# A planned four-layer graph kernel: new planning costs, groups of two at both ends, the last scores ranked ahead, and one late batch's variances on ScalarE

## The chip, the cores and the metric

The kernel runs on one core of a Trainium2 chip, in float32. The metric is device time in microseconds (us) of one execution; the time of a kernel is the median of its runs. The core's engines are TensorE (PE; its weight loads are listed as PEld), VectorE (DVE), ScalarE (ACT), GpSimd (POOL) and SyncE (SP), which here only issues transfers.

## The reference

There are 128 batches; each is a matrix x of 128 nodes by 512 features. All share one 128x128 adjacency matrix `adj`. Each batch passes through four layers, and each layer ends in a layer norm of x plus the layer's result:

```python
# layer 0: graph product
x = ln(x + (adj @ x) @ W0 + bias0)
# layer 1: graph attention; the mask multiplies the logits
h = x @ W;  s1, s2 = h @ a1, h @ a2
att = softmax(leaky_relu(s1[:, None] + s2[None, :], 0.2) * adj)
x = ln(x + elu(att @ h + beta * h))
# layer 2: max over features, one number for each node
A = adj @ x;  C = adj @ x + b
x = ln(x + max(relu(A[:, None, :] + (C - A)[:, :, None]), axis=-1))
# layer 3: 8 heads of 64, masked where adj is 0
q, k, v = split(x @ w_qkv)
o = softmax(where(adj == 0, -inf, q @ k.T / 8)) @ v
o = o @ w_proj + b_proj
x = ln(x + o + (o - mean(o)) * rsqrt(var(o) + eps) * gamma + beta)
```

So layer 3 has two norms, one of the projection `o` and one of the sum. A norm needs the mean and variance of 512 numbers in each of 128 rows, and a root.

## The kernel before, in words

**Data.** One batch is one 128x512 tile `x`; 18 tiles of it are in flight. The weights stay in SBUF. A 128x512 product is four matmuls over the inner dimension into one PSUM bank (`product`, L229), and each float32 matmul shows as two instructions, so a product is 8 instructions. PSUM has 5 banks named `mm` and 3 named `tr`.

**Layers 0 to 2** (`batch`). `mixed` (L237) multiplies x with the transposed adjacency or attention matrix into a `tr` bank; ScalarE copies the result to `yT` (L248) and `product` multiplies it with W0 or W. VectorE adds (L671, L696, L699), `bn_stats` and `bn_aggr` (L177, L183) give mean and variance, GpSimd raises variance plus eps to the power -0.5 (L191, `root`), and the normalise runs on ScalarE (L211) or VectorE (L216). Layer 2 is one matmul pair with adj (L706) and a maximum (L709). The attention weights of layer 1 are made for two batches at once (`attention1`), with trips through DRAM.

**Layer 3 works in groups** (`Group`): batches 0 to 115 in groups of four, 116 to 127 in six groups of two. When the x of a batch is done it is transposed by VectorE in blocks (L721) and taken through DRAM into the group's `xT` (`features`, four DMAs for each batch, L648). Once every batch of the group is there, `query_key` makes queries and keys for the whole group (L535; moving side 512 wide in a group of four, 256 in a group of two); ScalarE and VectorE copy them out (L544, L546). `tiled` then issues the score matmuls (L590) and, for groups of four, the attention matmuls of the group before (L611) in between; for the last groups each batch has its own score step and `attend` issues the attention matmuls. The softmax in between is mask add (L735), maximum (L742), eight exponentials on ScalarE (L746), a division (L753), a blocked transpose (L756) and two DMAs through DRAM (`p_d`). `values` makes v (a `product`). The attended rows are copied by ScalarE (L776) and projected. `usual` then does the two last norms: add of the bias (L795), statistics, two products on VectorE (L802, L805), statistics, normalise (L216), and the store from SP's queue (L809). `last` does the same for batch 127 in two half-width products (L824, L839, L840, L848, L854, L858, L863), so that its norm starts earlier.

**Slots.** `xT` and `qkT` (queries, keys, and then the softmax) have two slots each, one for each group; `v` has 8, `yT` 4, `ex` 2. The `xT` slot of a group comes free when its query-key work and all its `values` are done; the `qkT` slot when its attention matmuls are done.

**Order.** The order of every engine's queue is written out at build time by a planner in Python (`Plan`); on the chip each queue runs in that order, and an instruction waits for its inputs. Each step of a chain is requested with `use(engine, work, take, late, urgent, follow)`: the engine, the planned duration in us, the slots that it takes, what passes until its result may be used. The planner takes the request that can start first; among those that could start at the same time, `follow` goes before `urgent` before the rest, and then the lower rank:

```python
t, _, _, n = min(
    (self.at(r), r["want"][4], r["rank"], n) for n, r in enumerate(self.requests)
)
```

A TensorE request that is not `follow` is planned up to `MARGIN = 1.0` us after its inputs are ready. The rank is in general the batch's number (the group's first batch for group steps); `values` has its batch plus `LATER = 12`, and the layers 0 to 2 of the last 14 batches have 8 less. The planned durations do not exist on the chip: they only decide the order.

Of the kernel before, what the change touches and what calls it, by code (L numbers as in the profile page):

```python
# [8 lines left out]
F32 = mybir.dt.float32  # L9
# [7 lines left out]
D = 512  # L17
K = D // P
G = 4
PAIRS = 6  # L20
H = 8
HD = D // H
S = 32
# [22 lines left out]
class Plan:  # L46
# [15 lines left out]
    def use(self, engine, work, take=None, late=0.05, urgent=False, follow=False):  # L62

        names = take if callable(take) else lambda: (take,) if take else ()
        return engine, work, names, late, 0 if follow else 1 if urgent else 2
# [61 lines left out]
def gnn_stack_kernel(  # L131
# [40 lines left out]

    def mean_rstd(src):

        yield use("DVE", 1.03)
        st = small.tile([P, 6], F32, name="st")
        nc.vector.bn_stats(st, src)  # L177
        mv, ve = mean_var(st)
        return mv, (yield from root(ve))
# [14 lines left out]
    def beside(chain, rank):  # L194

        event, result = Event(), []

        def run():
            result.append((yield from chain))
            done(event)  # L200

        plan.start(run(), rank)
        return event, result

    def layernorm_act(xb):
        mv, rstd = yield from mean_rstd(xb)
# [24 lines left out]

    def mixed(xb, nodes, first=False):

        b0, b1 = yield use("PE", 0.91, lambda: ("tr", "yT"), late=0.2)
        p = bank([P, K, P], "tr")
        for k in range(K):
            nc.tensor.matmul(p[:, k, :], xb[:, k * P : (k + 1) * P], nodes, start=True, stop=True)  # L237
        yT = buf([P, K, P], "yT")
        if first:
            fill(2)  # L240

            yield use("DVE", 0.35, late=0.0)
            nc.vector.tensor_copy(yT[:, : K // 2], p[:, : K // 2])  # L243
            yield use("ACT", 0.05, urgent=True)
            nc.scalar.copy(yT[:, K // 2 :], p[:, K // 2 :])
        else:
            yield use("ACT", 0.6, urgent=True)
            nc.scalar.copy(yT, p)  # L248
        give(b0)
        return yT, b1  # L250
# [11 lines left out]
    make_identity(nc, ident)  # L262
    neghalf = const.tile([P, 1], F32, name="neghalf")
    nc.gpsimd.memset(neghalf, -0.5)
    adj_sb = const.tile([P, P], F32, name="adj_sb")
    adjT = const.tile([P, P], F32, name="adjT")

# [157 lines left out]

        return i - AHEAD if i >= NB - LAST else i

    quads = NB // G - PAIRS * 2 // G
    groups = {}

    def group(i):

        g = i // G if i < quads * G else quads + (i - quads * G) // 2
        if g not in groups:
            first, size = (g * G, G) if g < quads else (quads * G + (g - quads) * 2, 2)
            gr = groups[g] = Group(first, size)
            rank = first
            for h in range(size // 2):
                plan.start(attention1(gr, h), early(first + 2 * h))
            steps = K // gr.chunks  # L440
            for n in range(2 * steps):
                plan.start(query_key(gr, n // 2 * gr.chunks + K * (n % 2)), rank + n / K)


            if g < quads:
                plan.start(tiled(gr, groups.get(g - 1), range(size)), rank)
            else:
                for b in range(size):
                    plan.start(tiled(gr, None, (b,)), rank)
            if g >= quads - 1:  # L450
                for b in range(0, size, 2):
                    for bs in ((b, b + 1),) if g < quads + PAIRS - 1 else ((b,), (b + 1,)):
                        plan.start(attend(gr, bs), rank)
        return groups[g]


# [65 lines left out]
    def query_key(gr, c):  # L522
        yield gr.turned
        yield w3_in
        got = yield use("PE", 3.46, lambda: ("mm",) if gr.qkT else ("mm", "qkT"), late=0.2)
        if gr.qkT is None:
            bp, gr.slot["qkT"] = got
            gr.qkT = buf([P, G, 2 * K, P], "qkT")
        else:
            bp = got  # L530
        n = gr.chunks
        p = bank([P, n, gr.size * P], "mm")
        for j in range(n):
            for k in range(K):
                nc.tensor.matmul(  # L535
                    p[:, j, :], wqkv_sb[:, k, (c + j) * P : (c + j + 1) * P],
                    gr.xT[:, k, : gr.size * P], start=(k == 0), stop=(k == K - 1),
                )
        gr.read("xT", gr.size + 2 * K // n)
        yield use("ACT" if c < K else "DVE", 0.69, urgent=True)  # L540
        for j in range(n):
            dst = gr.qkT[:, : gr.size, c + j, :]
            if c < K:
                nc.scalar.mul(dst, p[:, j, :].rearrange("p (b n) -> p b n", b=gr.size), HD**-0.5)  # L544
            else:
                nc.vector.tensor_copy(  # L546
                    dst.rearrange("p b (c r) -> p b c r", c=Q),
                    p[:, j, :].rearrange("p (b r c) -> p b c r", b=gr.size, c=Q),
                )
        give(bp)  # L550
        done(gr.qk)

    def tiled(gr, before, bs):
        yield gr.qk
        waiting = list(range(before.size)) if before else []
        for b in waiting:
            yield before.rows[b]
        for n in range(0, len(bs), 2):

            now, then = bs[n : n + 2], waiting[: BUFS["tr"]]  # L560
            got = yield use(
                "PE", 0.1 + 0.88 * len(now) + 0.15 + 0.87 * len(then),
                lambda: ("mm", "mm") * len(now) + ("tr",) * len(then),
                late=0.0, urgent=True, follow=n > 0,
            )
            got = got if isinstance(got, list) else [got]
            for b in now:
                score(gr, b, got[:2])
                got = got[2:]
            if then:  # L570
                attends(before, then, got)

            for k, b in enumerate(now):
                done(
                    gr.scored[b],
                    0.15 - 0.88 * (len(now) - 1 - k) - (0.15 + 0.87 * len(then) if then else 0),
                )
            waiting = waiting[len(then) :]
            while waiting:
                got = yield use("PE", 0.88, "tr", late=0.0, follow=True)  # L580
                attends(before, waiting[:1], [got])
                waiting = waiting[1:]

# [12 lines left out]
    def attend(gr, bs):  # L596
        for b in bs:
            yield gr.rows[b]
        slots = yield use(
            "PE", 0.25 + 0.88 * len(bs), lambda: ("tr",) * len(bs), late=0.0, urgent=True  # L600
        )
        attends(gr, bs, slots if len(bs) > 1 else [slots])

# [17 lines left out]
    def values(i, gr, event):  # L621
        b = i - gr.first
        yield gr.turned
        bp, bv = yield use("PE", 3.46, lambda: ("mm", "v"), late=0.2)
        p = product(
            lambda k: gr.xT[:, k, b * P : (b + 1) * P], lambda k: wqkv_sb[:, k, 2 * D :]
        )
        yield use("ACT", 0.6, urgent=True)
        event.v = buf([P, D], "v")
        nc.scalar.copy(event.v, p)  # L630
        give(bp)
        gr.read("xT", gr.size + 2 * K // gr.chunks)
        event.slot = bv
        done(event)
# [19 lines left out]
    def batch(i):  # L654
# [8 lines left out]
        biased = Event()  # L663
        plan.start(pool_add(xb, bias0_sb, biased, bias0_in), i)
        yield w0_chunk[1]
        bp = yield use("PE", 3.46, "mm", late=0.2)
        p = product(lambda k: yT[:, k, :], lambda k: w0_sb[:, k, :])
        give(by)
        yield biased
# [15 lines left out]
        yield gr.attention[h]  # L685
        yT, by = yield from mixed(xb, gr.eT[h][:, b % 2])
        gr.read(h, 2)
        bp = yield use("PE", 3.46, "mm", late=0.2)
        p = product(lambda k: yT[:, k, :], lambda k: w1_sb[:, k, :])
        give(by)  # L690

# [9 lines left out]
        yield from layernorm_act(xb)  # L701


        bp = yield use("PE", 0.88, "mm", late=0.2, urgent=True)
        p = bank([P, D], "mm")
        nc.tensor.matmul(p, adjT, xb, start=True, stop=True)  # L706
        yield use("DVE", 0.69, urgent=True)
# [36 lines left out]
        for j in range(H):  # L744
# [31 lines left out]
        nc.scalar.copy(oT, p)  # L776
        give(ba)

        yield from (last if i == NB - 1 else usual)(
            i, xb, oT, valued, biased  # L780
        )

# [5 lines left out]

    def usual(i, xb, oT, valued, biased):

        bp = yield use("PE", 3.46, "mm", late=0.2)
        p = product(lambda k: oT[:, k, :], lambda k: wproj_sb[:, k, :])
        yield use("DVE", 0.69, urgent=True)
        o = valued.v
# [14 lines left out]
        nc.sync.dma_start(out[i], xb)  # L809
        give(x_slot[i])  # L810

    def last(i, xb, oT, valued, biased):

        halves = [slice(h * D // 2, (h + 1) * D // 2) for h in range(2)]
# [3 lines left out]

        def multiply():
            for h, columns in enumerate(halves):  # L820
                bp = yield use("PE", 1.73, "mm", late=0.0, follow=h > 0)
                p = bank([P, D // 2], "mm")
                for k in range(K):
                    nc.tensor.matmul(  # L824
                        p, oT[:, k, :], wproj_sb[:, k, columns], start=(k == 0), stop=(k == K - 1)
                    )
                banks.append((p, bp))
                done(multiplied[h], 0.2)
            give(valued.slot)
# [79 lines left out]
```

## Time and profile before

| | before |
|---|---|
| median of 4 runs | 3251.77 us (3251.59 to 3252.37) |
| the profiled execution, its own time | 3252.96 us |
| its span, first to last instruction | 3251.2 us, 40319 instructions |
| granted TensorE clock, mean | 0.999 |
| TensorE busy | 3234.8 us, 12767 matmul instructions |
| VectorE busy | 2670.1 us |
| ScalarE busy | 1186.2 us |
| GpSimd busy | 953.6 us |
| share of the DMA engines taken by the data queue | 30.8% |

In the lines of the profile, "L229" is line 229 of the kernel's file; a group's line gives engine, operation, `out<-in` by tile names, the count, the busy time and the mean duration of one in ns, and the idle time before the group with what ended it. TensorE's busy time is pipelined and its ends are modelled. The steps from the start of one matmul to the start of the next are the better measure of its pace: 0.429 us for a 512-wide instruction of a product, 0.216 for a 256-wide one. Some matmul records are missing from the trace.

### The profile page before, as it was taken

How to read it: one execution, taken by the hardware profiler on the slowest of the kernel's cores; microseconds unless marked ns; L12 is line 12 of the kernel's file. 1: busy time of each engine (PE TensorE's matmuls, PEld its weight loads, DVE VectorE, ACT ScalarE, POOL GpSimd, SP SyncE). 2: the span in 40 equal slices, each digit the busy share in tenths (PEclk: the TensorE clock that was granted, in tenths of full speed). 3: DMA queues.
4: the chain of work that ended last, by engine and by line, in shares of the span. 5: the costliest groups of instructions: out<-in, count | busy, mean ns of one | idle time of the engine just before them, and what ended most of it. 6: DMA issues, size and time to landing. Idle time of an engine off the chain costs nothing.

```text
span 3251.2 us, 40319 instructions
## 1 busy us (share of the span) xinstructions
PE 3234.8 (99%) x12767; PEld 1714.0 (53%) x12767; DVE 2670.1 (82%) x5671; ACT 1186.2 (36%) x3469; POOL 953.6 (29%) x1032
## 2 busy tenths in 40 slices
PE   9999999999999999999999999999999999999998
PEld 5455555555555555555555555555555555555565
DVE  7987797877978779787797877978779787878877
ACT  3343343423434333343333342334423333333332
POOL 3313232322323223232232322323223232322322
PEclk9999999999999999999999999999999999999999
DMA  5233332233322333223232232322333222332332
GB/s 172 69 90 101 99 101 94 61 103 98 102 91 61 107 94 105 94 58 104 94 110 90 61 101 94 113 87 64 98 94 115 88 70 78 115 106 72 93 111 85
DMA packets 469893, 304.27 MB, mean 94 GB/s; under 512 B 319280, under 2 KB 401584, under 8 KB 469680
## 3 DMA queue, kind: packets, MB, share of 16 engines
q1 hardware_dynamic: 469536, 301.42, 30.8%
q8 instruction: 102, 1.67, 0.2%
q14 instruction: 111, 0.91, 0.1%
q10 hardware_dynamic: 144, 0.26, 0.0%
HBM read 158.93 MB, written 142.67 MB: 93 GB/s over the span
## 4 chain that ended last, share of the span: by engine, by line
PE 98%; DVE 1%; DMA 0%; POOL 0%; issue 0%; ACT 0%; POOLq 0%; DVEq 0%; SPq 0%; ACTq 0%
PE mm L229 53%; PE mm L535 27%; PE tr L237 7%; PE mm L590 4%; PE tr L611 4%; PE mm L706 3%; DMA p_d<-pt 0%; DVE st L177 0%; DVE x L805 0%; DVE t L802 0%; DMA e_d<-et 0%; DVE x L216 0%; DVE pt L756 0%; DVE qkT L753 0%; POOL rstd L191 0%
## 5 line engine op out<-in xcount | busy, mean ns | idle before, releaser
L229 PE MATMUL mm<-w_sb,yT 128*128 128x512 f32 x2048 | 902.3, 592 | 0.2 <-DVE yT L243 0.2
L535 PE MATMUL mm<-xT,wqkv_sb 128*128 128x512 f32 (+1 forms) x2240 | 888.7, 556 | 0.0
L191 POOL TENSOR_TENSOR rstd<-ve,neghalf 128x1 f32<-128x1 f32 x640 | 438.1, 684 | 1148.8 <-DVE ve L185 952.5
L535 PEld LDWEIGHTS mm<-xT,wqkv_sb 128*128 128x128 f32 x2240 | 425.1, 190 | 455.6 <-issue 424.2
L229 PEld LDWEIGHTS mm<-w_sb,yT 128*128 128x128 f32 x2048 | 386.9, 190 | 475.5 <-issue 469.9
L229 PE MATMUL mm<-wqkv_sb,xT 128*128 128x512 f32 x1024 | 459.6, 593 | 0.0
L229 PE MATMUL mm<-wproj_sb,v 128*128 128x512 f32 x1016 | 444.4, 594 | 0.7 <-ACT v L776 0.7
L746 ACT ACTIVATE qkT<-qkT,nmx 128x128 f32<-128x128 f32 x1024 | 395.4, 390 | 40.0 <-DVE nmx L742 40.0
L222 POOL TENSOR_TENSOR x<-x,v 128x512 f32<-128x512 f32 x127 | 175.8, 1385 | 673.9 <-DVE v L795 672.1
L177 DVE BATCH_NORM_STATS2 st<-x 128x6 f32<-128x512 f32 x511 | 348.7, 682 | 4.8 <-ACT x L714 1.9
L229 PEld LDWEIGHTS mm<-wproj_sb,v 128*128 128x128 f32 x1016 | 191.2, 190 | 235.6 <-issue 230.3
L211 ACT ACTIVATE x<-x,nmr,rstd 128x512 f32<-128x512 f32 x256 | 205.3, 810 | 249.0 <-DVE nmr L209 245.9
L229 PEld LDWEIGHTS mm<-wqkv_sb,xT 128*128 128x128 f32 x1024 | 188.0, 190 | 203.7 <-issue 199.7
L544 ACT ACTIVATE qkT<-mm 128x512 f32<-128x512 f32 (+1 forms) x140 | 77.1, 560 | 558.1 <-PE mm L535 556.3
L222 POOL TENSOR_TENSOR x<-x,bias_sb 128x512 f32<-128x512 f32 x128 | 172.2, 1351 | 313.3 <-PE tr L237 303.6
L248 ACT COPY yT<-tr 128x512 f32<-128x512 f32 x255 | 148.5, 584 | 285.9 <-PE tr L237 285.8
L735 DVE TENSOR_TENSOR qkT<-mm,maskb 128x512 f32<-128x512 f32 x256 | 163.7, 684 | 80.1 <-PE mm L590 80.0
L222 POOL TENSOR_TENSOR x<-x,beta_sb 128x512 f32<-128x512 f32 x128 | 172.3, 1348 | 155.9 <-DVE xt L721 146.4
L678 DVE SCALAR_TENSOR_TENSOR scr<-x,wa_rows 128x512 f32<-128x512 f32 x256 | 194.9, 761 | 22.2 <-ACT x L211 17.5
L746 ACT ACTIVATION_READ_ACCUMULATOR qkT<-qkT,nmx 128x1 f32 x1024 | 194.4, 190 | 0.0
L694 ACT ACTIVATE ex<-mm 128x512 f32<-128x512 f32 x128 | 76.4, 597 | 299.3 <-PE mm L229 281.7
L630 ACT COPY v<-mm 128x512 f32<-128x512 f32 x128 | 74.9, 585 | 298.8 <-PE mm L229 298.2
(75 smaller groups left out, 3593.8 us busy)
## 6 DMA issues: line engine op xcount, KB each, us to landing
p_d<-pt SPq DMA_DIRECT2D x128, 512.0 KB
qkT<-p_d SPq DMA_DIRECT2D x128, 512.0 KB
x_d<-xt SPq DMA_DIRECT2D x128, 256.0 KB
xT<-x_d SPq DMA_DIRECT2D x512, 64.0 KB
x<-in_x SPq DMA_DIRECT2D x127, 256.0 KB
out<-x SPq DMA_DIRECT2D x127, 256.0 KB
z<-s_d SPq DMA_DIRECT2D x64, 128.0 KB
e_d<-et SPq DMA_DIRECT2D x64, 128.0 KB
```

Source lines behind the costliest of these rows:

```text
L177: nc.vector.bn_stats(st, src)
L191: nc.gpsimd.tensor_tensor(rstd, ve, neghalf, op=ALU.pow)
L211: nc.scalar.activation(xb, xb, AF.Identity, bias=nmr, scale=rstd)
L222: nc.gpsimd.tensor_tensor(dst, dst, other, op=ALU.add)
L229: nc.tensor.matmul(p, lhs(k), rhs(k), start=(k == 0), stop=(k == K - 1))
L237: nc.tensor.matmul(p[:, k, :], xb[:, k * P : (k + 1) * P], nodes, start=True, stop=True)
L248: nc.scalar.copy(yT, p)
L535: nc.tensor.matmul(p[:, j, :], wqkv_sb[:, k, (c + j) * P : (c + j + 1) * P], gr.xT[:, k, : gr.size * P], start=(k == 0), stop=(k == K - 1),)
L590: nc.tensor.matmul(p[j][:, c, :], gr.qkT[rws, b, c, :], gr.qkT[rws, b, K + c, :], start=True, stop=True,)
L678: nc.vector.scalar_tensor_tensor(scr, xb, 1.0, wa_rows[:, j, :], op0=ALU.mult, op1=ALU.mult, accum_out=gr.s[:, b, j : j + 1],)
L735: nc.vector.tensor_tensor(pr[:, j * K : (j + 1) * K], sc[j], maskb[:, None, :].to_broadcast([P, K, P]), op=ALU.add,)
L746: nc.scalar.activation(pr[:, j, :], pr[:, j, :], AF.Exp, bias=nmx[:, j : j + 1], accum_out=sums[:, j : j + 1],)
```

## The change

It has five parts.

1. The planned durations of TensorE steps are changed: a product from 3.46 to 3.44 us, `mixed` from 0.91 to 0.9, the 128x512 adjacency product and the score and attention steps from 0.88 to 0.87, and the statistics step on VectorE from 1.03 to 1.02.
2. The groups: two groups of two (batches 0 to 3), 29 groups of four (4 to 119), four groups of two (120 to 127).
3. The query-key and score steps of the last two groups (batches 124 to 127) get a rank lower by 8. Their attention steps keep theirs.
4. Batch 125 takes a new path, `late`, in place of `usual`: sums come from the `accum_out` of VectorE's products, the squares are summed by a `Square` on ScalarE, the last normalise runs on ScalarE, and the store is issued from ScalarE's queue.
5. A constant tile `eps` is set by GpSimd at the start.

The core of the diff (left out: lines where only a planned duration of part 1 changes):

```diff
-PAIRS = 6
+FIRST, PAIRS = 2, 4
+ENDING, SOON = 4, 8
...
+    def negated_mean(total):
+        nm = small.tile([P, 1], F32, name="nm")
+        nc.vector.tensor_scalar(nm, total, -1.0 / D, None, op0=ALU.mult)
+        return nm
+
+    def rstd_act(src, nm):
+
+        b = yield use("ACT", 1.2, "yT")
+        square = buf([P, D], "yT")
+        var = small.tile([P, 1], F32, name="var")
+        nc.scalar.activation(square, src, AF.Square, bias=nm, accum_out=var)
+        give(b)
+        ve = small.tile([P, 1], F32, name="ve")
+        nc.scalar.activation(ve, var, AF.Identity, bias=eps, scale=1.0 / D)
+        return (yield from root(ve, follow=True))
...
+    eps = const.tile([P, 1], F32, name="eps")
+    nc.gpsimd.memset(eps, EPS)
...
-    quads = NB // G - PAIRS * 2 // G
+    sizes = [2] * FIRST + [G] * ((NB - 2 * (FIRST + PAIRS)) // G) + [2] * PAIRS
+    firsts = [sum(sizes[:g]) for g in range(len(sizes))]
+    group_of = [g for g, size in enumerate(sizes) for _ in range(size)]
...
-        g = i // G if i < quads * G else quads + (i - quads * G) // 2
+        g = group_of[i]
         if g not in groups:
-            first, size = (g * G, G) if g < quads else (quads * G + (g - quads) * 2, 2)
+            first, size = firsts[g], sizes[g]
             gr = groups[g] = Group(first, size)
-            rank = first
+            rank = first - (SOON if first >= NB - ENDING else 0)
...
-            if g < quads:
+            joined = len(sizes) - PAIRS
+            if g < joined:
                 plan.start(tiled(gr, groups.get(g - 1), range(size)), rank)
             else:
                 for b in range(size):
                     plan.start(tiled(gr, None, (b,)), rank)
-            if g >= quads - 1:
+            if g >= joined - 1:
                 for b in range(0, size, 2):
-                    for bs in ((b, b + 1),) if g < quads + PAIRS - 1 else ((b,), (b + 1,)):
-                        plan.start(attend(gr, bs), rank)
+                    for bs in ((b, b + 1),) if g < len(sizes) - 1 else ((b,), (b + 1,)):
+                        plan.start(attend(gr, bs), first)
...
-        yield from (last if i == NB - 1 else usual)(
+        yield from (last if i == NB - 1 else late if i == NB - 3 else usual)(
             i, xb, oT, valued, biased
         )
...
+    def late(i, xb, oT, valued, biased):
+
+        bp = yield use("PE", 3.44, "mm", late=0.2)
+        p = product(lambda k: oT[:, k, :], lambda k: wproj_sb[:, k, :])
+        yield use("DVE", 0.92, late=0.0, urgent=True)
+        o = valued.v
+        total = small.tile([P, 2], F32, name="total")
+        nc.vector.scalar_tensor_tensor(
+            o, p, 1.0, bproj_sb, op0=ALU.mult, op1=ALU.add, accum_out=total[:, 0:1]
+        )
+        nm = negated_mean(total[:, 0:1])
+        give(bp)
+        added = yield from add_rows(xb, o, biased, i)
+        rooted, rstd = beside(rstd_act(o, nm), i)
+        b_t1 = yield use("DVE", 0.78, "ex")
+        t1 = buf([P, D], "ex")
+        nc.vector.scalar_tensor_tensor(t1, o, nm, gamma_sb, op0=ALU.add, op1=ALU.mult)
+        give(valued.slot)
+        yield added
+        yield rooted
+        yield use("DVE", 1.05)
+        nc.vector.scalar_tensor_tensor(
+            xb, t1, rstd[0], xb, op0=ALU.mult, op1=ALU.add, accum_out=total[:, 1:2]
+        )
+        nm = negated_mean(total[:, 1:2])
+        give(b_t1)
+        rstd = yield from rstd_act(xb, nm)
+        yield use("DVE", 0.21, follow=True)
+        nmr = small.tile([P, 1], F32, name="nmr")
+        nc.vector.tensor_scalar(nmr, nm, rstd, None, op0=ALU.mult)
+        yield use("ACT", 0.81)
+        nc.scalar.activation(xb, xb, AF.Identity, bias=nmr, scale=rstd)
+        yield use("ACT", 0.5, late=3.0)
+        nc.scalar.dma_start(out[i], xb)
+        give(x_slot[i])
```

In the changed kernel the engine of a `use` and its duration stand beside the instructions that it issues, as before.

More of the change, by code (lines that the diff above doesn't have):

```diff
@@ L173, in mean_rstd @@
     def mean_rstd(src):
-        yield use("DVE", 1.03)
+        yield use("DVE", 1.02)
         st = small.tile([P, 6], F32, name="st")
@@ L232, in mixed @@
     def mixed(xb, nodes, first=False):
-        b0, b1 = yield use("PE", 0.91, lambda: ("tr", "yT"), late=0.2)
+        b0, b1 = yield use("PE", 0.9, lambda: ("tr", "yT"), late=0.2)
         p = bank([P, K, P], "tr")
@@ L524, in query_key @@
         yield w3_in
-        got = yield use("PE", 3.46, lambda: ("mm",) if gr.qkT else ("mm", "qkT"), late=0.2)
+        got = yield use("PE", 3.44, lambda: ("mm",) if gr.qkT else ("mm", "qkT"), late=0.2)
         if gr.qkT is None:
@@ L561, in tiled @@
             got = yield use(
-                "PE", 0.1 + 0.88 * len(now) + 0.15 + 0.87 * len(then),
+                "PE", 0.25 + 0.87 * (len(now) + len(then)),
                 lambda: ("mm", "mm") * len(now) + ("tr",) * len(then),
@@ L575, in tiled @@
                     gr.scored[b],
-                    0.15 - 0.88 * (len(now) - 1 - k) - (0.15 + 0.87 * len(then) if then else 0),
+                    0.15 - 0.87 * (len(now) - 1 - k) - (0.15 + 0.87 * len(then) if then else 0),
                 )
@@ L579, in tiled @@
             while waiting:
-                got = yield use("PE", 0.88, "tr", late=0.0, follow=True)
+                got = yield use("PE", 0.87, "tr", late=0.0, follow=True)
                 attends(before, waiting[:1], [got])
@@ L599, in attend @@
         slots = yield use(
-            "PE", 0.25 + 0.88 * len(bs), lambda: ("tr",) * len(bs), late=0.0, urgent=True
+            "PE", 0.25 + 0.87 * len(bs), lambda: ("tr",) * len(bs), late=0.0, urgent=True
         )
@@ L623, in values @@
         yield gr.turned
-        bp, bv = yield use("PE", 3.46, lambda: ("mm", "v"), late=0.2)
+        bp, bv = yield use("PE", 3.44, lambda: ("mm", "v"), late=0.2)
         p = product(
@@ L665, in batch @@
         yield w0_chunk[1]
-        bp = yield use("PE", 3.46, "mm", late=0.2)
+        bp = yield use("PE", 3.44, "mm", late=0.2)
         p = product(lambda k: yT[:, k, :], lambda k: w0_sb[:, k, :])
@@ L687, in batch @@
         gr.read(h, 2)
-        bp = yield use("PE", 3.46, "mm", late=0.2)
+        bp = yield use("PE", 3.44, "mm", late=0.2)
         p = product(lambda k: yT[:, k, :], lambda k: w1_sb[:, k, :])
@@ L701, in batch @@
         yield from layernorm_act(xb)
-        bp = yield use("PE", 0.88, "mm", late=0.2, urgent=True)
+        bp = yield use("PE", 0.87, "mm", late=0.2, urgent=True)
         p = bank([P, D], "mm")
@@ L789, in usual @@
     def usual(i, xb, oT, valued, biased):
-        bp = yield use("PE", 3.46, "mm", late=0.2)
+        bp = yield use("PE", 3.44, "mm", late=0.2)
         p = product(lambda k: oT[:, k, :], lambda k: wproj_sb[:, k, :])
@@ L810, in usual @@
         give(x_slot[i])
+    def late(i, xb, oT, valued, biased):
+        bp = yield use("PE", 3.44, "mm", late=0.2)
+        p = product(lambda k: oT[:, k, :], lambda k: wproj_sb[:, k, :])
[30 more added lines that the diff above has]
+        give(x_slot[i])
     def last(i, xb, oT, valued, biased):
@@ L820, in multiply @@
             for h, columns in enumerate(halves):
-                bp = yield use("PE", 1.73, "mm", late=0.0, follow=h > 0)
+                bp = yield use("PE", 1.72, "mm", late=0.0, follow=h > 0)
                 p = bank([P, D // 2], "mm")
```

## The prediction

> **What bounds the kernel now.** I read the page's first part, then TensorE's waits, then the chain that ended last (all of it, then only 3221 to 3252 us), then a table by stretches, then single rows.
>
> ```profile
> span 3251.2 us, 40319 instructions
> PE 3234.8 (99%) x12767; PEld 1714.0 (53%) x12767; DVE 2670.1 (82%) x5671; ACT 1186.2 (36%) x3469; POOL 953.6 (29%) x1032
> ...
> PE tr L353 <- POOL ident masks.py:199: 1.4, 1, 1.4
> PE mm L706 <- ACT x L211: 0.8, 1, 0.8
> PE mm L824 <- ACT v L776: 0.7, 1, 0.7
> PE mm L229 <- ACT v L776: 0.7, 1, 0.7
> PE tr L237 <- DMA eT<-e_d: 0.6, 1, 0.6
> PE mm L229 <- DVE yT L243: 0.2, 1, 0.2
> ```
>
> TensorE is busy for 3234.8 of 3251.2 us, so all that a new order can win is 16.4 us. The waits (total, times, longest) name 4.4 of it; the other 12 are the tail after the last matmul. The first 1.4 us and the 0.2 are the start-up, which the change leaves alone.
>
> ```profile
> 3220.95 7.31 PE mm L229 x17
> 3228.28 0.70 DVE v L795
> 3229.01 0.70 DVE st L177
> 3230.11 0.83 DVE t L802
> ...
> 3236.80 0.69 DVE v L795
> ...
> 3239.82 0.75 DVE x L805
> ```
>
> This is the chain that ended last, in its final 30 us. It leaves TensorE at 3228.28, 11 us before TensorE's last matmul, when the projections of batches 124 and 125 are done. From there VectorE's layer norms of 124 to 127 set the end, with short steps on GpSimd. The table by stretches says the same (PE, PEld, DVE, ACT, POOL busy):
>
> ```profile
> 124.00:128.00 4.00, 3.19 (x9) 1.17 (x8) 3.90 (x12) 1.72 (x3) 1.26 (x1) 1.00 0.31 90
> ...
> 460.00:3228.00 2768.00, 2768.00 (x10972) 1467.16 (x10970) 2276.44 (x4800) 1014.50 (x2993) 809.55 (x870) 1.00 0.31 91
> 3228.00:3239.30 11.30, 9.79 (x57) 6.13 (x56) 9.99 (x21) 1.17 (x2) 5.58 (x7) 1.00 0.40 128
> 3239.30:3251.20 11.90, 0.00 (x0) 0.00 (x0) 7.32 (x19) 0.00 (x0) 4.04 (x6) 0.63 0.12 45
> ```
>
> For 2768 us TensorE never waits. In the last matmuls VectorE is busy 9.99 of 11.30 us while ScalarE has 1.17.
>
> **The change part by part.** The profiled execution took 3252.96 us: its span of 3251.18 and 1.8 us around it. The median of the runs is 3251.77, 1.2 below it; I sum on the span and take the sum from the median.
>
> *Groups of two at the start, four pairs at the end in place of six.* There are six pairs before and after, so the matmuls are the same: a pair's query-key work steps 64 times by 0.216 us (13.81 us), as much of a quad's 32 times by 0.429 (13.73). The 24 half-width copies on ScalarE and VectorE, and the DMAs by batch, stay as many. What moves is when the first query-key product can start. Before, it needs four batches turned: it starts at 127.5, just behind the 0.81 us gap at 124.9, with VectorE busy 3.90 of 4.00 us. With two batches it needs batches 0 and 1 alone, whose copies to xT are issued at 99.9 and 109.3; 13.8 us of TensorE work is then at hand by about 115. The gap goes: -0.8 (0 to -0.8).
>
> *Score blocks.* The step before a run of score or attention matmuls takes 0.523 instead of 0.429, and the second one behind it 0.533: 0.2 us for each run. In TensorE's timeline I count 41 runs: 2 for the first quad, 28 for the joined quads, 11 at the end. After: 1 for each of the first pairs, 29 for the quads, some 8 at the end, 39 in all. Two fewer: -0.4 (0 to -0.8).
>
> *Measured durations.* A product steps 8 times by 0.429 us, 3.43 us; the plan said 3.46 and now says 3.44. This emits no instruction and shifts the order within queues everywhere. It is hidden while TensorE has ready work, as in the 2768 us. The one other gap, 0.65 at 458.4 (a DMA's landing), is drawn anew: -0.3 (0 to -0.65).
>
> *Last scores ahead.* Query-key and score steps of 124 to 127 pass the projections of 120 to 123 in rank. Before, the last query-key work ran from 3189.4 to 3203.2 and the last scores at 3206.7; their softmax, two round trips through DRAM (0.3 to 0.45 us of SP's queue for each issue, ahead of some output stores) and attention reach TensorE at 3228.3 and 3233.7 with nothing left beside them: the two gaps of 0.73 and 0.74 are projections that wait for ScalarE's copy of the attended rows. How much earlier can they be? The copies to xT of 126 and 127 are issued by 3161; the query-key slots are two, and the pair before the last frees one with its attention at 3178.5. So the query-key product can move from 3189 to about 3178, and the scores by some 11 us, not 20. That still puts four projections and more behind them, which cover both gaps: -1.5 (-0.7 to -1.5, the nearer row being the gaps themselves). If that cover is gone, the 1.5 us are back.
>
> *Batch 125 on ScalarE.* VectorE loses, by the rows of 3228 to 3237: 0.69 + (0.69 + 0.18 + 0.15) + 0.75 + 0.75 + (0.68 + 0.18 + 0.15) + 0.54 = 4.8 us. It gains two products with a sum (bounds 0.68 by L696 without one, and 0.76 + 0.08 by L678 with its accumulator read; I take 0.84), one without (0.75), two negated means (0.15 each by L185) and one nmr (0.20): 2.9. So 1.9 us leave VectorE. ScalarE gains, for each variance, a Square that the trace does not have: 0.72 (L714, one pointer) to 0.81 (L211, two), its accumulator read 0.19, and a 128x1 Identity between 0.19 and 0.39; twice 1.2 to 1.3, a 0.81 normalise and a DMA issue (0.41 on its queue; SP's loses one). About 3.7 us, beside 1.17 us of work in 11.3. GpSimd keeps both roots and gets one 0.1 us memset at the start, behind the identity. The new wait: each Square, and the last normalise, sit in ScalarE's queue waiting for VectorE or GpSimd; behind them may stand the copies of 126 and 127 (L776), which release their projections. Their idle time before is 6.6 and 4.9 us, so I charge nothing; without that cover about 1 us for each.
>
> The row on tables: one ACT_TABLE_LOAD in the whole run, 1.28 us, for Copy, Exp and Identity. [...]
>
> *What the end gains from that.* TensorE ends at 3239.29. A projection's add follows its product by 0.2 us (3224.65 to 3224.85), but the last half's add starts only at 3242.28, held by the norms of 124 to 126: 2.8 us late. From that add to the end it is 8.9 us, unchanged. With 1.9 us less on VectorE and the softmax of 126 and 127 off it sooner, I take -1.8 (-0.5 to -2.8).
>
> Sum: 0.8 + 0.4 + 0.3 + 1.5 + 1.8 = 4.8 us. 3251.77 - 4.8 = 3247.0 (span about 3246.4).
>
> **The rivals.** About 0.2% (6.5 us, 3245.3 and 3258.3) is what a measurement of this kernel can tell from no change.
>
> *Faster: every term at its upper end.* 0.81 + 0.65 + 0.8 + 1.47 + 2.8 = 6.5 us: 3245.2, just over the line. For it: none of these gaps has a reason to stay if the order is good. Against: it needs all five.
>
> *The rank does not bite.* The last query-key product waits for slots and landings and not for its rank, so the two gaps and part of the norms' delay stay: 0.8 + 0.4 + 0.3 + 1.0 = 2.5 us, 3249.3. For it: two xT and two query-key slots, each held by the pairs before. Against: 11 us between the slot's release and the product.
>
> *Slower: TensorE runs dry at about 140 to 160 us.* Two pairs fill both xT slots with four batches instead of eight, and a slot comes free only after the values products, which rank 12 behind. Then features of 4 to 7 go out: 4 x 2.6 us of SP issue and at most 3.8 until they are used (123.3 to 127.1), 14.2 us without query-key work. If nothing else is ready, that replaces the 0.8: 14.2 - 4.0 = 10.2 us slower, 3262.0; it passes the line once the gap is over 10.5. Against: before, there was no query-key work from 187 to 257 while the values of 0 to 3 ran as late as 205 to 231, and TensorE did not wait.
>
> **How the numbers follow.** Forecast 0.43, faster rival 0.25, rank without effect 0.20, dry TensorE 0.12. So faster 0.25, same 0.63, slower 0.12. The range takes the faster rival and a little under it, 3244.5, and above it no gain at all, 3252.0; beyond are the slower rival and a few in a hundred below.
>
> **What would show it.** Right: no wait of TensorE near 125 us; the last scores some 10 us earlier against the end; no waits for L776; the last half's add within 1 us of its product; one table load; ScalarE's Square near 0.75 us. Wrong: new TensorE waits between 130 and 260 us, table loads beside Square, a copy of 126 or 127 queued behind a Square, or the chain leaving TensorE earlier than 11 us before its last matmul.

## The result, and the profile after

| | before | after |
|---|---|---|
| median, all runs | 3252.22 us (3251.21 to 3254.4, 60 runs) | 3256.47 us (3254.29 to 3258.83, 42 runs) |
| span of the profiled execution | 3251.18 us | 3254.53 us |
| last matmul ends | 3239.28 us | 3245.15 us |
| from there to the end | 11.9 us | 9.4 us |

The changed kernel takes 1.0013 of the time before, with a 95% interval of 1.0008 to 1.0017: slower, by less than the 0.2% of the text above, but outside the range of 3244.5 to 3252.0, and on the other side of no change than the 3247.0 forecast.

The page's first part, and TensorE's waits in the changed kernel (engine and line, released by: us in total, times, longest):

```profile
span 3254.5 us, 40265 instructions
PE 3237.3 (99%) x12767; PEld 1713.3 (53%) x12767; DVE 2656.5 (82%) x5669; ACT 1182.3 (36%) x3476; POOL 960.3 (30%) x1033
...
PE mm L728 <- ACT x L228: 1.8, 3, 0.6
PE mm L246 <- ACT v L798: 1.7, 1, 1.7
PE tr L372 <- POOL ident masks.py:199: 1.4, 1, 1.4
PE mm L882 <- ACT v L798: 1.3, 1, 1.3
PE tr L254 <- DMA eT<-e_d: 1.2, 2, 0.7
PE mm L246 <- DVE yT L260: 0.3, 1, 0.3
```

The gap of 0.81 us near 125 us is gone. New are seven gaps (3.1 us; the five longest are in the rows above) between 887 and 2304 us, where the adjacency product waits for ScalarE's normalise and `mixed` for the landing of eT, the attention weights that come back from DRAM. And the two waits at the end have not gone but grown, from 0.73 and 0.74 to 1.72 and 1.27 us. TensorE's count of matmuls is the same, yet it is busy for 2.5 us more. The chain that ended last (start, length, what) shows the new link in the end:

```profile
3231.03 0.71 DVE v L841 x2
3231.74 0.02 issue
3231.77 0.16 DVE nm L208
...
3232.01 0.82 ACT yT L216 x2
...
3232.92 0.29 ACT ve L219
3233.22 0.48 ACT v L798
3233.70 0.04 issue
3233.74 5.41 PE mm L246 x8
```

L798 is ScalarE's copy of batch 126's attended rows. It starts when batch 125's Square (L216) and the Identity behind it (L219) are through: it stood behind them in the queue. Experiments 1 and 3 test whether that order costs the time. And the projection that it releases takes 5.41 us in place of 3.70. The table by stretches says why (the eighth column, 1.00, 0.50 and 0.65, is the granted clock):

```profile
3232.00:3234.00 2.00, 0.28 (x3) 0.26 (x2) 1.90 (x2) 1.58 (x4) 2.00 (x2) 1.00 0.23 45
3234.00:3236.00 2.00, 2.00 (x3) 0.71 (x3) 1.93 (x6) 0.00 (x0) 0.66 (x1) 0.50 0.62 218
3236.00:3238.00 2.00, 2.00 (x4) 0.86 (x3) 1.28 (x4) 1.10 (x3) 0.92 (x1) 0.65 0.04 8
```

After the wait of 1.72 us the clock is granted at half, 0.50, for 3.4 us, and matmuls step by 0.853 us instead of 0.429. "Busy" hides that.

### The profile page after: what moved, and what is told of

Same layout as the page of the kernel before. It is cut to its first block, busy times and chain, and to the rows that moved or that the text cites. A ratio compares the mean times of both kernels' runs of the same rounds, so it can differ in the third digit from the quotient of the medians.

```text
span 3254.5 us, 40265 instructions
## 1 busy us (share of the span) xinstructions
PE 3237.3 (99%) x12767; PEld 1713.3 (53%) x12767; DVE 2656.5 (82%) x5669; ACT 1182.3 (36%) x3476; POOL 960.3 (30%) x1033
## 4 chain that ended last, share of the span: by engine, by line
PE 98%; DVE 1%; DMA 0%; POOL 0%; ACT 0%; issue 0%; SPq 0%; POOLq 0%; DVEq 0%; ACTq 0%
PE mm L246 53%; PE mm L557 27%; PE tr L254 7%; PE mm L612 4%; PE tr L633 4%; PE mm L728 3%; DVE st L178 0%; DVE e L528 0%; DMA p_d<-pt 0%; DVE x L233 0%; DMA eT<-e_d 0%; POOL rstd L192 0%; DMA e_d<-et 0%; PE tr L372 0%; DVE mv L184 0%
## 5 line engine op out<-in xcount | busy, mean ns | idle before, releaser
L239 POOL TENSOR_TENSOR x<-x,bias_sb 128x512 f32<-128x512 f32 x128 | 179.4, 1408 | 189.1 <-PE tr L254 179.3
```

What stands on the lines that cost most here:

```text
L239: nc.gpsimd.tensor_tensor(dst, dst, other, op=ALU.add)
```

## The experiments

Time is given as the median beside that of the kernel before on the same chip (3252.1 to 3252.3 in all of them). Lines of a profile are those of each kernel's own file; the names of tiles are the same.

**1. Batch 125 back on VectorE (e1).** The changed kernel, with

```diff
-(last if i == NB - 1 else late if i == NB - 3 else usual)
+(last if i == NB - 1 else usual)
```

> The changed kernel with batch 125 on the usual path (variances on VectorE). Queue theory: the copies of the attended rows of 126 and 127 no longer stand behind a Square or the last normalise of 125 in ScalarE's queue, so the wait of 1.72 us before projection 126 falls to about 0.7, TensorE stays at 0.429 us a step there (1.85 us back) and the wait before projection 127 falls from 1.27 to about 0.7: TensorE's last matmul 3 to 3.5 us earlier (3241.7). VectorE's tail grows again by up to 1.9 us: 1.5 to 3.5 us faster than the changed kernel in all. Rival (batch 125 on ScalarE is a gain and the loss comes from the other parts): about 2 us slower than the changed kernel.

3255.82 us. The waits for the copy are the old 0.7 each, there is no half-rate stretch, and the last matmul ends at 3242.17, 3.0 us earlier than in the changed kernel:

```profile
PE mm L246 <- ACT v L798: 0.7, 1, 0.7
PE mm L882 <- ACT v L798: 0.7, 1, 0.7
```

Behind it stand 11.8 us again instead of 9.4. So this part of the change gained 2.4 us behind the last matmul and lost 3.0 ahead of it. The queue theory holds for the waits; the time fell by 0.65 us and not by the 1.5 to 3.5 expected, which is within the spread of these kernels' runs, so for the time the part is worth nothing that can be told.

**2. The half clock alone (e2).** In the changed kernel, behind the attention matmuls of 126:

```diff
+            warm = bank([P, K, P], "tr")
+            for n in range(16):
+                nc.tensor.transpose(warm[:, n % K, :], ident, ident)
```

> The changed kernel with 16 transposes of the identity (0.107 us each at the full rate, 1.7 us) on TensorE behind the attention matmuls of batch 126, into a spare bank that nothing reads; every other queue keeps its order. Clock theory (a wait of 1.72 us halves TensorE's rate for some 4.8 us): the projection of 126 still starts at the same time but steps by 0.429 us, it ends 1.85 us earlier, and the end comes about 1.8 us earlier. Rival (the slow steps come from what runs beside them, such as VectorE or the landing DMA): steps of 0.853 us stay and the time is the same within 0.3 us.

3256.19 us. TensorE's timeline (start, length, instructions, idle before and releaser):

```profile
3234.49 1.97 PE L631 MATMUL tr<-ident 128*128 128x128 f32 x16
3236.29 3.69 PE L246 MATMUL mm<-wproj_sb,v 128*128 128x512 f32 x8
3239.91 1.10 PE L641 MATMUL tr<-qkT,v 128*64 128x128 f32 x16
3242.82 5.41 PE L890 MATMUL mm<-wproj_sb,v 128*128 128x256 f32 x16 [1.81 <-ACT v L806]
```

With filler in the gap, and everything beside it as before, the projection runs at full rate: 3.69 us instead of 5.40. The clock theory holds for the stretch. (The profiled execution is the slowest of the eleven: its times here are 2.5 us later than those of the changed kernel, with 1.9 us more of waits in the middle.) The time did not follow, 0.3 us instead of 1.8: ScalarE still held the copy of 127 behind 125's normalise, so the next wait grew from 1.27 to 1.81 us and the half rate fell on the last product, 5.41 us in place of 3.72. The 4.8 us of the expectation are set right by the changed kernel's trace: its clock is at half for 3.4 us.

**3. The copies ahead in ScalarE's queue (e5), and batch 125 alone on the kernel before (e7).** e5 plans 125's first Square 1.2 us and its last normalise 1.5 us later (`late=1.2`, `late=1.5` on the VectorE steps ahead of them):

> The changed kernel, with batch 125 still on ScalarE, but planned later by 1.2 us (first Square) and 1.5 us (last normalise), so that in ScalarE's queue the copy of batch 126 stands ahead of the first Square and the copy of 127 ahead of the normalise. Queue theory: both waits for the copy fall to about 0.74 us as with 125 on VectorE (e1), no half-rate stretch, last matmul at about 3242.2; and the tail behind it stays at the changed kernel's 9.4 us. So span 3251.6, 2.5 to 3 us faster than the changed kernel (median about 3253.6). Rival (what e1 won at the matmuls came from something else that 125's path does, or the delay of 125 lengthens the tail to 11.8): the same as e1, 3255.8, within 0.5.

3255.5 us, 1.0 less than the changed kernel and not 2.5 to 3; by the time alone it is the rival that came, within 0.5 us of e1. The waits are 0.74 and 1.06, no half rate, last matmul at 3243.08; the tail, the time behind the last matmul, is 10.2 us, between e1 and the changed kernel. The wait for the first copy fell as expected. The copy of 127 now stands ahead of the normalise, but still behind batch 125's second Square, and waits 0.3 us more than in e1; the tail gave back 0.8 us.

> The kernel before with nothing but batch 125 on ScalarE (old durations, groups, ranks). In this order too the copies of 126 and 127 stand behind a Square and behind the normalise of 125 on ScalarE. Queue theory: the waits of 0.73 and 0.74 us before the last two projections grow to about 1.7 and 1.3 to 2, with a half-rate stretch behind any over 1.5: 1.5 to 5 us more until the last matmul, against 2.0 to 2.5 us less behind it: between 0.5 us faster and 2.5 us slower than the kernel before. Rival (VectorE's 1.9 us are what counts): 1.5 to 2 us faster.

e7: 3252.78 us beside 3252.10 (1.0002, interval 0.9993 to 1.0011). In TensorE's timeline:

```profile
3229.59 3.70 PE L246 MATMUL mm<-wproj_sb,v 128*128 128x512 f32 x8 [1.63 <-ACT v L798]
3233.22 1.09 PE L633 MATMUL tr<-qkT,v 128*64 128x128 f32 x16
3236.65 5.41 PE L882 MATMUL mm<-wproj_sb,v 128*128 128x256 f32 x16 [2.34 <-ACT v L798]
```

The same trade in the old order: 2.8 us later at the last matmul, 3.0 us less behind it, and a time that cannot be told from that of the kernel before. The 1.5 us of the expectation, a value between the 1.27 and 1.72 us of the changed kernel, was an estimate that no run bears out as a limit: behind 1.63 us here the product took 3.70 us, behind 2.34 us 5.41.

**4. The rank of the last scores (e4, e8).** `SOON = 0` in the changed kernel, and `SOON = 8` alone on the kernel before:

> The changed kernel with the query-key and score steps of 124 to 127 at their old rank. If the rank has brought the last attention matmuls forward: the waits at the end grow, 1 to 3 us slower. If it only moved the scores and the softmax then waited behind the norms of 120 to 123 on VectorE: the attention of 126 comes at the same distance from the end, and the time is the same within 1 us. In this order both copies of 126 and 127 stand behind the whole of batch 125 in ScalarE's queue, so the wait for them should be longer than 1.72 us and the slow steps stay.

> The kernel before with nothing but the lower rank for query-key and score steps of 124 to 127. The last scores come earlier by about 7 to 10 us, but the order of the last five steps on TensorE (attention 126, projection 126, attention 127, projection 127) is as before with nothing in between. If the waits come from that order: 0.73 and 0.74 us stay, and the time is within 0.7 us of the kernel before. If they come from late scores, as I had predicted: both waits go, 1.5 us faster or more. If the rank matters here as in e4 (12 us): it would be much faster, which only a long wait in the kernel before could give, and there is none.

e4: 3268.05 us, 11.6 slower than the changed kernel, which neither expectation had: attention 126 waits 8.7 us for its softmax to land. The wait for the copy is 1.58 us, not longer than 1.72. e8: 3263.42, 11.3 slower than the kernel before: there the rank does harm, by a wait of attention 127:

```profile
PE tr L633 <- DMA qkT<-p_d: 11.2, 1, 11.2
```

Neither theory of e8 had that. VectorE's timeline of e8 shows where batch 127's softmax was:

```profile
3226.63 1.23 DVE L775 TENSOR_TENSOR qkT<-qkT,rs 128x1024 f32<-128x1024 f32 x1
3228.02 0.69 DVE L817 TENSOR_TENSOR v<-mm,bproj_sb 128x512 f32<-128x512 f32 x1 [0.17 <-PE mm L246]
...
3235.97 0.69 DVE L817 TENSOR_TENSOR v<-mm,bproj_sb 128x512 f32<-128x512 f32 x1
3236.58 1.23 DVE L778 STREAM_TRANSPOSE pt<-qkT 128x1024 f32<-128x1024 f32 x1
```

The division is done at 3227.9; the transpose comes 8.7 us later, behind the norms of 124 to 126. The scores had been ranked ahead, the softmax steps on VectorE had not: with rank 127 they go last.

**5. The softmax ranked ahead too (e9, e10, e11).** From the scores to the returned rows, for the last four batches:

```diff
         yield gr.scored[b]
+        yield i - 8 if i >= NB - 4 else i
...
         done(gr.rows[b])
+        yield i
```

> The kernel before with the lower rank for the last query-key and score steps (as e8) and, new, a rank lower by 8 for the softmax steps of batches 124 to 127 as well, until their rows are back. Theory: e8's wait of 11.2 us for batch 127 came from VectorE's queue, where its division and transpose (rank 127) were planned behind the norms of 124 to 126; with the softmax ahead the attention of 126 and 127 is one run ahead of projection 125, whose 3.4 us hide ScalarE's two copies. So no wait of over 0.2 us for the copy or the landing at the end, last matmul 1.5 us earlier than before (3237.8), some 13 us faster than e8, and 0 to 2 us faster than the kernel before (the norms of 124 to 127 come closer together, so VectorE's tail stays at about 11.9). Rival (two slots for scores and softmax limit it, not the rank): a wait of several us for the landing stays.

> As e9, with batch 125 on ScalarE as in the change. Both copies of 126 and 127 now stand ahead of its first Square. Queue theory: nothing waits behind a Square, so this path gives what e7 showed behind the last matmul (8.9 to 9.4 in place of 11.9 us) and costs TensorE nothing: 2 to 3 us faster than e9, last matmul at 3237.8, span about 3247, 3 to 5 us faster than the kernel before. Rival (VectorE gets no shorter path because three norms are late together): the same as e9 within 0.7 us.

> The changed kernel with the softmax of 124 to 127 ranked ahead by 8 and batch 125 planned later on ScalarE as in e5, so that both copies stand ahead of the first Square. If the end of the changed kernel was spoiled by these two orders and nothing else: no waits at the end, no half-rate stretch, last matmul 1.5 to 2 us before that of e5 (3241.3), tail 9 to 9.4, span about 3250.5; the eight waits in the middle stay. 4 us faster than the changed kernel, 0 to 2 us faster than the kernel before. If the end has a third cause: more than 3252.

e9: 3251.62 us, 11.8 less than e8. Both attention steps now stand ahead of projection 125, and nothing waits at the end; the last matmul ends at 3236.63, but 13.2 us follow, and the time is not told apart from that of the kernel before (0.9998, interval 0.9989 to 1.0007). That the longer tail comes from VectorE having three norms at once was expected, not tested. e10 adds batch 125 on ScalarE: 3249.34 beside 3252.14 (0.9991, interval 0.9982 to 1.0000), the last matmul at 3235.57 and 11.0 us behind it. TensorE's waits in e10, all of them, and its end:

```profile
PE tr L372 <- POOL ident masks.py:199: 1.4, 1, 1.4
PE mm L728 <- ACT x L228: 0.8, 1, 0.8
PE mm L246 <- DVE yT L260: 0.3, 1, 0.3
...
3223.08 1.97 PE L633 MATMUL tr<-qkT,v 128*64 128x128 f32 x32
3224.98 7.13 PE L246 MATMUL mm<-wproj_sb,v 128*128 128x512 f32 x16
3231.95 3.62 PE L884 MATMUL mm<-wproj_sb,v 128*128 128x256 f32 x16
```

That is 2.8 us, of the 3.3 that I had predicted of the rank and the end together, with an interval that just reaches no change: it takes both, and the softmax's rank with them. e11, the same on the changed kernel with e5's later Square: 3254.0, 2.5 less than the changed kernel and not the 4 expected; its end has one wait of 0.32 us, and the middle kept its eight waits, 4.9 us in its profile (the 4.3 us in the expectations of experiment 7 was counted too low).

**6. Groups and planned durations (e3, e6, e12).** Old durations; groups of four at the start (`FIRST, PAIRS = 0, 4`); `MARGIN = 1.5`. Each is one kind of edit of the changed kernel:

> The changed kernel with the old planned durations (3.46, 0.91, 0.88, 1.03); groups, ranks and batch 125 as changed. Cost theory (the exact durations leave the plan no reserve, so that waits for ScalarE's normalise and for a DMA's landing come back every 700 us): the 2.6 to 3.1 us of waits at 888, 1568, 1595 and 2302 us shrink to the 1.5 of the kernel before or less, 1 to 2 us faster than the changed kernel. Rival (the shifted groups make these waits): they stay, within 0.5 us.

> The changed kernel with groups of four at the start (batches 0 to 119) and the four pairs at the end, new durations, ranks and batch 125 as changed. If the pairs at the start make the waits in the middle (888 to 2304 us, eight gaps, 3.1 us): they go, the 0.8 us gap near 125 us comes back, 1.5 to 2.5 us faster than the changed kernel. If the new durations make them: gaps of the same kind and sum (2 to 4 us) stand at other places, and the time is the same within 1 us or slower by the 0.8.

> The changed kernel with TensorE's requests planned up to 1.5 us after their inputs are ready in place of 1.0. Only the middle (200 to 3100 us) is of interest, since the order of the end is drawn anew. If the waits at 888, 1568, 1595 and 2302 us (ScalarE's normalise 0.59 us late, a DMA's landing 0.1 to 0.7 us late) come from a plan that leaves too little reserve now that its products are short: they fall below 0.6 us in all. If they come from the order that the groups force: they stay at 2 us or more.

e3: 3296.13 us, 40 slower, and both theories miss. None of the waits at 888 to 2304 us is there; others are, above all 33 us at the end:

```profile
PE tr L633 <- DMA qkT<-p_d: 32.8, 3, 25.0
PE mm L557 <- DVE mx L731: 2.4, 1, 2.4
```

e6: 3269.03, 12.6 slower, where at most 1 us had been expected. The waits in the middle stand at other places with the same spacing of some 707 us (490, 1198, 1905, 2612), the gap near 125 us is 3.3 us, and one of 5.0 us comes at 2723. So the middle waits do not come from the pairs at the start. The gap near 125 us is in the kernels whose first group is of four and in none that starts with pairs, so the pairs do remove it; how much of the 12.6 us they are worth is open, for the rest of the order changed too. e12: 3259.52 us, 3.1 slower than the changed kernel; the waits in the middle stay (2.9 us), in other shares, and one of 2.8 us for a landing comes at the end. A larger margin is no cure. The new durations with the old groups were not tried.

**7. Which duration (e13, e14, e15).** Each takes e11 and sets one kind of planned duration back: the product to 3.46, `mixed` and the adjacency product to 0.91 and 0.88, the statistics to 1.03. They have few runs: two of e13, eight of e14, three of e15.

> The kernel of e11 (changed, softmax of 124 to 127 and the copies ahead) with the planned product back at 3.46 and every other new duration kept. Read in the middle only (200 to 3100 us): if the product's duration makes the waits at 888, 1568, 1595 and 2304 us, the three of 0.58 for ScalarE's normalise go and the sum of gaps falls from 4.3 us in e11 to under 1. If another of the new durations does, they stay.

> The kernel of e11 with the old durations for the two short steps before and after the products (mixed 0.91, adjacency product 0.88) and the new ones for all others. The step that waits is one of these two (the adjacency product for ScalarE, mixed for a landing): if their own planned length makes the waits, they go (under 1 us in the middle); if not, they stay at 2 us or more.

> The kernel of e11 with the statistics step on VectorE planned at 1.03 as before in place of 1.02, all else as e11. There are five such steps for each batch, so VectorE's plan is 0.05 us in 25 longer. If a VectorE plan that is too short makes ScalarE's normalise come 0.58 us late, the three waits for it go; if not, they stay and the middle keeps 2 us or more.

e14: 3249.32 us beside 3252.12 (0.9992, interval 0.9981 to 1.0003), 4.7 less than e11; the waits in the middle are gone but for one landing, and the gap near 125 us as well:

```profile
PE tr L254 <- DMA eT<-e_d: 1.7, 1, 1.7
PE tr L372 <- POOL ident masks.py:199: 1.4, 1, 1.4
```

e13: 3291.28 us, with 33 us of gaps; e15: 3271.21, with 17. With each of the three edits the waits of 0.58 us at their old places go, so no one duration is shown to make them. And 0.02 or 0.01 us on other steps bring other waits, up to ten times as long in all, which no outcome written down for e13 and e15 had. The traces show more: in e1, e2, e4, e5 and e11, which leave the durations alone, the three waits of 0.59 us for ScalarE come back at the same places, while the order of ScalarE's queue in e3, e13, e14 and e15 leaves that of the changed kernel within the first 100 us. A duration is less a cause than a new draw of 40000 instructions' order. What decides a draw is open.

## Why the prediction was wrong, step by step

Three steps failed: the new durations were taken as hidden, the rank of the scores was taken to bring the attention forward, and batch 125's work on ScalarE was charged with no wait.

**The bound** was right: TensorE, and behind its last matmul VectorE. The time could only move by gaps, by TensorE's rate and by the tail, and it did.

**Groups of two at the start**, -0.8: right; the gap near 125 us went.

**Score blocks**, -0.4: wrong by all of it. The changed kernel has 41 runs, as before: of the late ones fewer merged than I had counted.

**Measured durations**, -0.3 (0 to -0.65): this is the term that failed most. I priced it by the gaps that the old order had, and called it hidden because TensorE had not waited for 2768 us. But that quiet was a property of one order, and every order is drawn anew. What came is seven new gaps of 3.1 us, with an estimated 0.2 us of restart at each (e1 ends its matmuls 2.9 us later than before, with the same two waits at the end and 1.9 us more of gaps ahead of them), against 0.65 saved. Nor was that 0.65 us the order's own: e7, e9 and e10 run the kernel before in the same order up to the last batches, and their profiles do not have it; it was a late landing in that execution. Whether the new gaps come of the durations or of the groups the runs do not part: e3, with the old durations and the new groups, has other gaps and worse. The bounds should have reached above zero, and far: e3, e13 and e15 lie 15 to 40 us up. No rival had this either; the one of a dry TensorE at 140 to 160 us did not come.

**Last scores ahead**, -1.5: failed. The scores did come 10 us earlier against the last matmul (42.5 us instead of 32.5), though 3.2 of it are only the longer end: in e1, whose end is as before, it is 39.3. The attention of 126 did not: its distance to the last matmul is the same 11.0 us in the kernel before and in e1. What I missed is that each later step has a rank of its own, and that VectorE, as e8 shows, puts batch 127's softmax behind the norms of 124 to 126. In e9, where the softmax has the rank too, both waits are gone, the 1.5 us predicted; but TensorE's gain was lost again behind the last matmul, and only e10 is faster. My rival of a rank without effect named slots and landings; it had the outcome of e1's end and the wrong cause. The rank mattered all the same: without it the changed kernel's order has 11.6 us more (e4).

**Batch 125 on ScalarE**: the prices were right (Square 0.72 us, VectorE's part 2.8 against my 2.9, and the whole profile has one ACT_TABLE_LOAD, of 1.28 us, as the kernel before has without Square). The wait was named, copies of 126 and 127 behind a Square, and charged with nothing, for ScalarE's idle time before. That idle time says nothing of when the Square comes. The Square is released by the add behind projection 125, the copy by the attention matmuls that TensorE runs right after that projection, and in the changed kernel the two were ready within 0.1 us of each other (3232.01 and 3232.02 us). So the step charged at nothing measured 3.2 us: 1.0 and 0.5 us more of waits, which my fallback of about 1 us for each came near, and 1.7 us of half rate behind the first, which it lacked.

**The end**, -1.8: right in sign and near in size, 2.5 us by the profiled executions, in part by luck: TensorE's last product came late, and VectorE, which was to set the end, stood idle for 1.7 us waiting for projection 126. Where TensorE is less delayed, the path on ScalarE took 1.6 us (e5 beside e1) and 2.2 us (e10 beside e9) off the time behind the last matmul.

Sum by the profiles: middle +2.6 (3.1 and restarts, less the gaps at 125 and 458 us with theirs), waits at the end +1.5, half rate +1.7, tail -2.5: 3.3 of the measured 3.35 us. The medians differ by 4.25, because the profiled execution of the kernel before took 0.7 us more than its median (3252.96 beside 3252.22) and that of the changed kernel 0.15 less (3256.32). The landing waits in the middle vary between executions (3.1 us of gaps in this profile, 5.0 in e2's, with the same order), which may be what moves single executions; that is argued, not shown.

## What to carry to other kernels

When a program's queues are written out from a plan, a change of its numbers is not a small edit: price it by several draws on the chip, not by the gaps of the old one. When a step is to come earlier, move the rank of everything between it and its last reader, on every engine. And before work moves to an idle engine, ask which short instruction there is awaited by the bound engine at that same moment: put it ahead in the queue, or the gain is paid back.

## What the runs showed of the hardware

In the changed kernel TensorE's granted clock was 0.50 from 3234.00 to 3237.41, behind the single wait of 1.72 us, and the product there took 5.40 us, 1.7 more than the 3.70 of the same product in the kernel before. Behind 1.81 us (e2) and 2.34 us (e7) the next product took 5.41 us. Behind 1.27 us (changed kernel) and 1.63 (e7) it took 3.72 and 3.70. But the length of the wait alone does not decide: behind 1.73 us in e14, and 1.72 and 1.80 in e6, the next product took 3.60, 3.70 and 3.72 us (the first two lines are e14's, the others e6's):

```profile
862.63 2.02 PE L254 MATMUL tr<-eT,x 128*128 128x128 f32 x16 [1.73 <-DMA eT<-e_d]
864.49 3.60 PE L246 MATMUL mm<-w_sb,yT 128*128 128x512 f32 x8
...
3249.00 3.70 PE L246 MATMUL mm<-wproj_sb,v 128*128 128x512 f32 x8 [1.72 <-ACT v L798]
...
3255.52 3.72 PE L882 MATMUL mm<-wproj_sb,v 128*128 128x256 f32 x16 [1.80 <-ACT v L798]
```

In the changed kernel's trace the granted clock is 1.00 from 3237.42 on and 0.50 again from 3247.65 to the end, 2.5 us after the end of the last matmul (3245.15). What parts the waits that cost the rate from those that do not is open: 1.72 us did in the changed kernel, 1.72 and 1.80 us did not in e6.

In the changed kernel, whose TensorE is busy for 99% of the span, the wait of 1.72 us cost 3.4 us in all: itself, and 1.7 us in the product behind it.
